# A cross-attention kernel's prologue: queries ahead of keys, x in three pieces, products of the identity, unit 0's maxima drawn together

## The chip, the cores and the metric

The kernel runs on one core of one Trainium2 chip. The metric is the device time of one launch in microseconds (us); of several runs the median is given. A profile is one execution taken by the hardware profiler. TensorE (PE) does matrix products, VectorE (DVE) and ScalarE (ACT) work on vectors, GpSimd (POOL) does elementwise work, SyncE (SP) issues DMAs. PEld is TensorE's weight load.

## The reference, cut to what matters

Two layers of cross attention are applied one after the other to x (32 sequences of 256 rows, 320 channels), each with its own weights. The context has 77 rows of 512 channels per sequence and is the same for both layers. The object, other and image-prompt slices of the reference start past row 77, so they are empty here and add nothing.

```python
q = _split_heads(hidden_states @ Wq.T, H)          # 20 heads of 16
k = _split_heads(text @ Wk.T, H)
v = _split_heads(text @ Wv.T, H)
out = _merge_heads(_attend(q, k, v, 1 / 4))        # softmax over 77 keys
return out @ Wo.T + bo + residual
```

Everything is in float32.

## The kernel before, in words

The work is cut into 32 units: 16 pairs of sequences times two layers, in the order of `units_in_order`. The first four units are layer 0 of pairs 0 to 3. Channels lie on partitions: x of a pair is a tile of 128 x 1280, channels 0 to 127 of both sequences in the first 512 columns, channels 128 to 255 in the next 512, and the last 64 channels of both sequences in the last 256 columns. A unit's 20 heads are handled in five groups (`of_group`).

For each unit the kernel makes:

- `keys` (L215) and `keys_rest` (L236): K transposed, in three banks of PSUM, moved to the tile kT by VectorE (L229) and ScalarE (L253), from which GpSimd makes kM (L256)
- `queries` (L258): the first 256 output channels in four banks. `last_channels` adds the products of the last 64 input channels and `main_channels` those of the first 256; ScalarE copies the banks to q0 (L268). `queries_rest` (L270) does the last 64 output channels and then copies q0 to q1 with a DMA from SP (L277)
- `maxima` (L319), once per group: products of queries and keys into four banks (psm), whose greatest entries VectorE reduces (L334, four reduces) into the tile max
- `turn` (L341): VectorE transposes the maxima (L343), and eight small DMAs (L347) write them into rows of q0 (e = 0, four DMAs) and q1 (e = 1, four DMAs), so that the next products take them off by themselves
- `scores` (L353), once per group: the products that need those rows (pss, L360, first q0, then q1), and the exponential on ScalarE (L366)
- `vals` (L284), `place_vals` (L302): V for a chunk of 128 context rows, and DMAs that put it where a unit needs it
- `values` (L409), `turn_back` (L412), `finish` (L428), `finish_rest` (L436): products with V, division, the output projection, bias and residual

The order of instructions on every engine is the order in which the program issues them. It is written out by hand: the function `at` puts a step in a slot and under a name, and L497 to L501 walk the slots, in each slot in the order load, maxima, turn, scores, values, rest, back, full, last. Unit u's scores start at slot 5u. Before them come its keys (slot s - 8, for unit 0 s - 9), queries (s - 9), keys_rest (s - 7), values (s - 6, s - 5), queries_rest (s - 5), maxima (s - 6 to s - 2) and turn (s - 2), with s = 5u. For units 0 and 1 these slots interleave in the prologue, slots -10 to 0, which is the stretch that the change touches.

Loads: SP's queue takes the context of unit 0, x of pair 0, and later context chunks, x and weights. ACT's queue takes the key, query and value weights of layer 0 (L131). All PSUM tiles come from one pool of eight banks, used in turn: a bank is taken again when the tile eight allocations back has been read. x has seven buffers, so the loads of the first pairs wait for no buffer. DMAs that SP or ACT issues stand in that engine's order of instructions[...].

The identity (L139, L140) is made by GpSimd before anything else is computed; VectorE makes the masks from it (L158 to L166).

Of the kernel before, what the change touches and what calls it, by code (L numbers as in the profile page):

```python
# [53 lines left out]
B, S, C, CA, L = 32, 256, 320, 512, 77  # L54
HEADS, HD = 20, 16
P = 128
NB = 2
NT = NB * S
NX = 2 * NT + S
# [9 lines left out]
PARTS, WIDE = {}, 0  # L69
# [21 lines left out]
def xattn_kernel(ctx: ExitStack, tc: tile.TileContext, xT, cT, cP, weights, outT):  # L91
    nc = tc.nc
# [10 lines left out]
    def bank(name):  # L103
        return psum.tile([P, 512], F32, tag="bank", name=name)
# [2 lines left out]

    def load_x(p):
        x_sb = io.tile([P, NX], F32, tag="x", name=f"x_{p}", bufs=AHEAD + 3)
        nc.sync.dma_start(out=x_sb, in_=xT[p])  # L110
        xs[p] = x_sb

    def load_context(u):
        p = units[u][0]
        c_sb = cs[u] = io.tile([P, NKA, NB * L], F32, tag="c", name=f"c_{u}", bufs=3)
        nc.sync.dma_start(out=c_sb, in_=cP[:, p])
# [10 lines left out]
    def load_weights(layer, first, last, queue):  # L127
        a = PARTS[first][0]
        at, rows, width = PARTS[last]
        b = at + rows * width  # L130
        queue.dma_start(out=w_sb[layer]["all"][:, a:b], in_=weights[layer][:, a:b])  # L131


    load_context(0)
    load_weights(0, "k", "k", nc.scalar)
    load_x(0)
    load_weights(0, "q", "q22", nc.scalar)

    ident = const.tile([P, P], F32, name="ident")  # L139
    make_identity(nc, ident)  # L140
# [23 lines left out]
    for e in range(2):  # L164
        i = HD * (1 - e)
        nc.vector.tensor_scalar_mul(less[:, e : e + 1], r32[:, i : i + 1], -1.0)  # L166

    st = [{} for _ in units]

# [13 lines left out]
    def last_channels(ps, w2, x, **flags):  # L183
        for t in range(2):
            for b in range(NB):
                r = slice(64 * b, 64 * b + 64)
                by_columns(
                    ps[t][b][:, 0:S], w2[r, 0, t * P : (t + 1) * P], x[r, 2 * NT : NX], **flags
                )

    def main_channels(ps, w, x, start, stop):
        for t in range(2):
            for kc in range(2):
                for b in range(NB):
                    i = kc * NT + b * S
                    by_columns(
                        ps[t][b][:, 0:S], w[:, kc, t * P : (t + 1) * P], x[:, i : i + S],
                        start=(start and kc == 0), stop=(stop and kc == 1),
                    )
# [15 lines left out]
    def keys(u):  # L215
        p, layer = units[u]
        w, c_sb = w_sb[layer], cs[u]
        kT = st[u]["k"] = work.tile([P, 2, NG, L], F32, tag="kT", name=f"kT_{u}", bufs=3)
        for t in range(2):
            ps = bank(f"psk_{u}_{t}")  # L220
            for kc in range(NKA):
                by_columns(
                    ps[:, 0 : 2 * L],
                    w["k"][:, kc, t * P : (t + 1) * P],
                    c_sb[:, kc, :],
                    start=(kc == 0),
                    stop=(kc == NKA - 1),
                )
            nc.vector.tensor_tensor(  # L229
                kT[:, :, 2 * t : 2 * t + 2].rearrange("p e g k -> p e (g k)"),  # L230
                ps[:, 0 : 2 * L].unsqueeze(1).broadcast_to([P, 2, 2 * L]),
                masks.unsqueeze(2).broadcast_to([P, 2, 2 * L]),
                ALU.mult,
            )

    def keys_rest(u):  # L236

        p, layer = units[u]
        w, c_sb = w_sb[layer], cs[u]
        kT = st[u]["k"]  # L240
        ps = bank(f"psk_{u}_2")
        for kc in range(NKA):
            for i in range(4):
                b, m = i // 2, i % 2
                nc.tensor.matmul(  # L245
                    ps[32 * i : 32 * i + 32, 0:L],
                    w["k"][:, kc, 2 * P + 32 * m : 2 * P + 32 * m + 32],
                    c_sb[:, kc, b * L : (b + 1) * L],
                    start=(kc == 0),
                    stop=(kc == NKA - 1),  # L250
                )
        for e in range(2):
            nc.scalar.activation(kT[:, e, 4], ps[:, 0:L], AF.Copy, scale=masks[:, e : e + 1])  # L253
        kM = st[u]["km"] = work.tile([P, 2, NG, L], F32, tag="kM", name=f"kM_{u}", bufs=3)
        for e in range(2):
            nc.gpsimd.tensor_scalar_add(kM[:, e], kT[:, e], less[:, e : e + 1])  # L256

    def queries(u):  # L258
        p, layer = units[u]
        w = w_sb[layer]  # L260
        q0, _ = st[u]["q"] = [
            work.tile([P, NX], F32, tag=f"q{e}", name=f"q{e}_{u}", bufs=3) for e in range(2)
        ]
        ps = [[bank(f"psq_{u}_{t}_{b}") for b in range(NB)] for t in range(2)]
        last_channels(ps, w["q2"], xs[p], start=True, stop=False)
        main_channels(ps, w["q"], xs[p], start=False, stop=True)
        for g in range(4):
            nc.scalar.copy(of_group(q0, g), ps[g // 2][g % 2][:, 0:S])  # L268

# [49 lines left out]
    def maxima(u, g):  # L319
        q0, kT, mx = st[u]["q"][0], st[u]["k"], maxes[u % 2]  # L320
        q = of_group(q0, g)
        ps = [bank(f"psm_{u}_{g}_{j}") for j in range(4)]
        for c in range(S // P):
            for j in range(4):
                r = slice(32 * j, 32 * j + 32)
                nc.tensor.matmul(  # L326
                    ps[j][:, c * 2 * L : (c + 1) * 2 * L],
                    q[r, c * P : (c + 1) * P],
                    kT[r, :, g, :],
                    start=True,  # L330
                    stop=True,
                )
        for j in range(4):
            nc.vector.tensor_reduce(  # L334
                mx[:, 2 * g : 2 * g + 2, 2 * j : 2 * j + 2],
                ps[j][:, : 4 * L].rearrange("p (c e k) -> p c e k", e=2, k=L),
                AX.X,
                ALU.max,
            )

    def turn(u):  # L341
        mT = work.tile([P, 2 * NG * 32], F32, tag="mT", name=f"mT_{u}", bufs=2)
        nc.vector.transpose(mT, maxes[u % 2].rearrange("p k i -> p (k i)"))  # L343
        for e in range(2):
            q = st[u]["q"][e].rearrange("(j i) n -> i j n", i=32)[HD * (1 - e)]
            for a in range(P // 32):
                nc.sync.dma_start(  # L347
                    out=q.rearrange("j (k a n) -> a j k n", a=P // 32, n=32)[a],
                    in_=mT[32 * a + e : 32 * a + 8 : 2].rearrange("j (k n) -> j k n", n=32),
                )  # L350
# [98 lines left out]
    def at(slot, where, step):  # L449
        place.setdefault((slot, where), []).append(step)  # L450

    made = [0, 0]
    for u, (p, layer) in enumerate(units):
        s = NG * u
        if layer == 0 and u > 0:
            at(s - 14, "load", lambda p=p: load_x(p))
        if u > 0:
            at(s - 12, "load", lambda u=u: load_context(u))
        at(s - 8 if u else s - 9, "rest", lambda u=u: keys(u))
        at(s - 9, "last", lambda u=u: queries(u))  # L460
        at(s - 7, "rest", lambda u=u: keys_rest(u))
        need = range(p * NB * L // P, ((p + 1) * NB * L - 1) // P + 1)
        when = s - 6
        for i in need:
            if i < made[layer]:
                at(when, "full", lambda u=u, i=i: place_vals(u, i))
                continue
            at(when - 3, "load", lambda layer=layer, i=i: load_chunk(layer, i))
            at(when, "full", lambda layer=layer, i=i: vals(layer, i))
            at(when, "full", lambda u=u, i=i: place_vals(u, i))  # L470
            made[layer] += 1
            when = s - 5
        at(s - 5, "rest", lambda u=u: queries_rest(u))
        for g in range(NG):
            at(s - 6 + g, "maxima", lambda u=u, g=g: maxima(u, g))
            at(s + g, "scores", lambda u=u, g=g: scores(u, g))
            at(s + g + 1, "values", lambda u=u, g=g: values(u, g))
            at(s + g + 1, "back", lambda u=u, g=g: turn_back(u, g))
        at(s - 2, "turn", lambda u=u: turn(u))
        if u < NU - 2:  # L480
            at(s + NG + 1, "full", lambda u=u: finish(u))
            at(s + NG + 3, "rest", lambda u=u: finish_rest(u))
        else:

            slot = NG * NU - (u == NU - 2)
            at(slot, "full", lambda u=u: finish(u))
            at(slot, "last", lambda u=u: finish_rest(u))


    at(-10, "load", lambda: load_weights(0, "v", "v", nc.scalar))  # L490
# [106 lines left out]
```

## Time and profile before

| | |
|---|---|
| median of three runs | 999.02 us (992.94, 999.02, 1000.55) |
| the profiled execution | 995.15 us, its span 993.4 us |
| TensorE busy | 977.5 us of the span, 98% |
| VectorE, ScalarE, GpSimd busy | 590.9, 421.7, 182.7 us |
| first product on TensorE | at 5.65 us |
| first scores of unit 0 | at 37.62 us (first half), 39.89 us (second half) |
| mean granted TensorE clock | 0.995 |
| DMA share, 5 to 10 us and 35 to 40 us | 1.03 and 0.05 |

How to read the lines below. In lists of waits, `A <- B: sum, times, longest` says that instructions A stood still until B had ended. In the chain of work that ended last, each line has a start, a duration and the group of instructions that the chain runs through; "SPq" is the issue of a DMA by SP, "DMA q<-mT" the time until such a transfer had landed, and x64 counts records, of which an fp32 product has two. In tables by window, the stretch is followed by its length, the busy time of the engine asked for, the granted clock, the share of time in which the DMA engines were busy, and the GB/s that they moved. `L173` is the helper that splits a product by columns, so the tile's name (psk, psq, psv, psy) tells keys, queries, values and output apart.

### The profile page before, as it was taken

The page shows a single profiled execution, that of the slowest core. Times are in us where ns is not written, and L with a number is a line of the kernel's source. Part 1 is how long each engine was busy: PE and PEld are TensorE (multiplying, and loading weights), DVE is VectorE, ACT ScalarE, POOL GpSimd, SP SyncE. Part 2 cuts the span into 40 slices and gives each one's busy share as a digit, 9 for nine tenths or more (in the row PEclk, how much of TensorE's full clock was granted, in tenths as well). Part 3 has the DMA queues.
Part 4 walks back from the last instruction along what each step waited for, and adds up shares of the span by engine and source line. Part 5 has one row for each costly group of instructions (what it writes and reads, how often), then busy time and mean ns, then how long its engine had stood idle before and what let it go on. Part 6 is the DMA issues. An engine that isn't in the chain of part 4 may idle for free.

```text
span 993.4 us, 43878 instructions
## 1 busy us (share of the span) xinstructions
PE 977.5 (98%) x19664; PEld 609.0 (61%) x19664; DVE 590.9 (59%) x1380; ACT 421.7 (42%) x905; POOL 182.7 (18%) x236
## 2 busy tenths in 40 slices
PE   7899999999999999999999999999999999999988
PEld 4566665666666666665666666666666666666644
DVE  2466555666655665655666656666556656556654
ACT  1344343454444443444444444444444534444442
POOL 2122201221202222112222112221022221122211
PEclk9999999999999999999999999999999999999989
DMA  6541222221132411223212232311323111231111
GB/s 213 177 160 37 74 79 97 70 77 62 57 122 70 132 47 60 92 80 122 71 44 85 68 123 70 122 34 53 121 80 119 50 62 54 69 107 48 58 47 54
DMA packets 53949, 83.59 MB, mean 84 GB/s; under 512 B 15556, under 2 KB 35652, under 8 KB 53762
## 3 DMA queue, kind: packets, MB, share of 16 engines
q1 hardware_dynamic: 53330, 78.96, 23.9%
q8 instruction: 154, 2.52, 1.0%
q10 hardware_dynamic: 432, 1.84, 0.5%
q14 instruction: 33, 0.27, 0.1%
HBM read 35.39 MB, written 10.49 MB: 46 GB/s over the span
## 4 chain that ended last, share of the span: by engine, by line
PE 97%; DVE 1%; DMA 1%; SPq 1%; issue 0%; POOL 0%; DVEq 0%; POOLq 0%
PE po L380 16%; PE pss L360 15%; PE psy L173 14%; PE psq L173 14%; PE psm L326 12%; PE psv L173 8%; PE psk L173 7%; PE psq L212 4%; PE psy L212 4%; PE psk L245 2%; SPq L347 1%; DVE max L334 1%; DMA w<-in_w_dram 0%; DMA q<-mT 0%; DVE mT L343 0%
## 5 line engine op out<-in xcount | busy, mean ns | idle before, releaser
L366 ACT ACTIVATE pT<-pss 77x512 f32<-77x512 f32 x640 | 326.9, 590 | 242.1 <-PE pss L360 242.1
L334 DVE TENSOR_REDUCE max<-psm 128x4 f32<-128x308 f32 x640 | 259.4, 466 | 172.1 <-PE psm L326 172.1
L401 POOL TENSOR_TENSOR normal<-turned,inv 128x256 f32<-128x256 f32 x160 | 99.3, 621 | 763.9 <-DVE inv L396 763.9
L360 PE MATMUL pss<-q,kM 32*77 32x256 f32 x2560 | 180.6, 380 | 5.8 <-DMA q<-mT 5.8
L380 PE MATMUL po<-pT,v 77*32 77x256 f32 x2560 | 174.0, 389 | 1.0 <-DVE max L334 1.0
L173 PE MATMUL psy<-oT,w 128*32 128x256 f32 (+1 forms) x3072 | 149.4, 380 | 0.0
L173 PE MATMUL psq<-x,w 128*32 128x256 f32 (+1 forms) x3072 | 149.4, 380 | 0.0
L392 DVE STREAM_TRANSPOSE turned<-po 128x512 f32<-128x512 f32 x160 | 113.3, 708 | 46.0 <-PE po L380 42.9
L268 ACT COPY q<-psq 128x256 f32<-128x256 f32 x128 | 47.6, 372 | 213.3 <-PE psq L173 209.5
L326 PE MATMUL psm<-kT,q 32*128 32x154 f32 x2560 | 129.1, 314 | 0.0
L360 PEld LDWEIGHTS pss<-q,kM 32*77 32x77 f32 x2560 | 114.4, 142 | 23.4 <-issue 10.6
L326 PEld LDWEIGHTS psm<-kT,q 32*128 32x128 f32 x2560 | 91.9, 183 | 55.3 <-issue 41.7
L380 PEld LDWEIGHTS po<-pT,v 77*32 77x32 f32 x2560 | 67.5, 110 | 90.3 <-DVE max L334 58.4
L415 DVE STREAM_TRANSPOSE oT<-normal 128x256 f32<-128x256 f32 x160 | 70.9, 443 | 84.5 <-POOL normal L401 81.4
L173 PEld LDWEIGHTS psq<-x,w 128*32 128x32 f32 (+1 forms) x3072 | 85.4, 109 | 57.6 <-issue 14.4
L173 PEld LDWEIGHTS psy<-oT,w 128*32 128x32 f32 (+1 forms) x3072 | 82.2, 108 | 61.2 <-issue 13.2
L422 DVE SCALAR_TENSOR_TENSOR x<-psy,w,x 128x256 f32<-128x256 f32 x160 | 68.6, 479 | 62.8 <-PE psy L173 56.4
L173 PE MATMUL psv<-w,cv 128*32 128x320 f32 x1232 | 93.5, 433 | 0.0
L256 POOL TENSOR_SCALAR kM<-kT,less 128x385 f32<-128x385 f32 x64 | 79.9, 1260 | 38.8 <-ACT kT L253 38.6
L173 PE MATMUL psk<-c,w 128*32 128x154 f32 x2048 | 75.2, 299 | 5.6 <-DMA w<-in_w_dram 5.6
L173 PEld LDWEIGHTS psk<-c,w 128*32 128x32 f32 x2048 | 67.0, 112 | 12.8 <-DMA w<-in_w_dram 5.6
L173 PEld LDWEIGHTS psv<-w,cv 128*32 128x32 f32 x1232 | 41.0, 110 | 40.6 <-issue 1.9
(24 smaller groups left out, 328.3 us busy)
## 6 DMA issues: line engine op xcount, KB each, us to landing
q<-q SPq DMA_DIRECT2D x32, 640.0 KB
x<-in_xT_dram SPq DMA_DIRECT2D x16, 640.0 KB
c<-in_cP_dram SPq DMA_DIRECT2D x32, 308.0 KB
cv<-in_cT_dram SPq DMA_DIRECT2D x38, 256.0 KB
out_dram<-x SPq DMA_DIRECT2D x15, 640.0 KB
v<-stage SPq DMA_DIRECT2D x26, 192.5 KB
q<-mT SPq DMA_DIRECT2D x256, 5.0 KB
w<-in_w_dram ACTq DMA_DIRECT2D x2, 640.0 KB
```

What stands on the lines that cost most here:

```text
L173: nc.tensor.matmul(out[m : m + 32], lhsT[:, m : m + 32], rhs, **flags)
L212: nc.tensor.matmul(ps[r, 0:S], lhsT, rhs, start=(kc == 0), stop=(kc == 2))
L256: nc.gpsimd.tensor_scalar_add(kM[:, e], kT[:, e], less[:, e : e + 1])
L326: nc.tensor.matmul(ps[j][:, c * 2 * L : (c + 1) * 2 * L], q[r, c * P : (c + 1) * P], kT[r, :, g, :], start=True, stop=True,)
L334: nc.vector.tensor_reduce(mx[:, 2 * g : 2 * g + 2, 2 * j : 2 * j + 2], ps[j][:, : 4 * L].rearrange("p (c e k) -> p c e k", e=2, k=L), AX.X ...
L360: nc.tensor.matmul(ps[j][:L, e * S : (e + 1) * S], kM[r, e, g, :], q[r, :], start=True, stop=True,)
L366: nc.scalar.activation(st[u]["p", g][j][:L], ps[j][:L], AF.Exp, scale=SCALE)
L380: nc.tensor.matmul(po[32 * j : 32 * j + 32, e * S : (e + 1) * S], vpad[:L, b, pair, e].rearrange("p a d -> p (a d)"), pT[j][:L, e * S : (e ...
L392: nc.vector.transpose(turned[:, 0 : 2 * S], po)
L401: nc.gpsimd.tensor_tensor(normal.rearrange("p q e d -> p e q d"), outs, inv.unsqueeze(3).broadcast_to([P, 2, S // 32, HD]), ALU.mult,)
L415: nc.vector.transpose(of_group(st[u]["o"], g), normal)
L422: nc.vector.scalar_tensor_tensor(x, ps[:, 0:S], w_sb[layer]["b"][:, 0, t : t + 1], x, ALU.add, ALU.add)
```

## The change

The change is confined to the prologue.

1. x of pair 0 is loaded first, on SP, in three pieces by columns (512, 512, 256), ahead of the context of unit 0. On ACT the query weights come first, in three pieces (two rows of 320 columns, then the rest), and the key weights behind them. x of pair 1 is issued by ACT instead of SP.
2. Four products of the identity with itself go to a bank of their own that nothing reads.
3. Unit 0's queries come before its keys (slot -10, then keys and keys_rest in slot -9), and in them the last channels come after the main ones.
4. Unit 0's maxima of groups 0 to 4 go from slots -6, -5, -4, -3, -2 to -6, -5, -4, -4, -3, and its turn from -2 to -3. Unit 1's keys and keys_rest go from slots -3 and -2 to -4, its queries from -4 to -3, behind the turn.
5. Of unit 0's eight small DMAs in `turn`, the last of each four is issued by ACT.

```diff
+        if p == 0:
+            for a, b in ((0, NT), (NT, 2 * NT), (2 * NT, NX)):
+                nc.sync.dma_start(out=x_sb[:, a:b], in_=xT[p, :, a:b])
+        else:
+            (nc.scalar if p == 1 else nc.sync).dma_start(out=x_sb, in_=xT[p])
...
+    load_x(0)
+    first, _, _ = PARTS["q"]
+    for i in range(2):
+        n = slice(first + i * C, first + (i + 1) * C)
+        nc.scalar.dma_start(out=w_sb[0]["all"][:, n], in_=weights[0][:, n])
+    load_weights(0, "q2", "q22", nc.scalar)
     load_context(0)
     load_weights(0, "k", "k", nc.scalar)
-    load_x(0)
-    load_weights(0, "q", "q22", nc.scalar)
...
+    warm = bank("warm")
+    for _ in range(4):
+        nc.tensor.matmul(warm[:, 0:P], ident, ident, start=True, stop=True)
...
-        last_channels(ps, w["q2"], xs[p], start=True, stop=False)
-        main_channels(ps, w["q"], xs[p], start=False, stop=True)
+        if u == 0:
+
+            main_channels(ps, w["q"], xs[p], start=True, stop=False)
+            last_channels(ps, w["q2"], xs[p], start=False, stop=True)
+        else:
+            last_channels(ps, w["q2"], xs[p], start=True, stop=False)
+            main_channels(ps, w["q"], xs[p], start=False, stop=True)
...
-                nc.sync.dma_start(
+                queue = nc.scalar if u == 0 and a == 3 else nc.sync
+                queue.dma_start(
...
-        at(s - 8 if u else s - 9, "rest", lambda u=u: keys(u))
-        at(s - 9, "last", lambda u=u: queries(u))
-        at(s - 7, "rest", lambda u=u: keys_rest(u))
+        if u > 1:
+            at(s - 8, "rest", lambda u=u: keys(u))
+            at(s - 9, "last", lambda u=u: queries(u))
+            at(s - 7, "rest", lambda u=u: keys_rest(u))
...
+            if u > 0:
+                at(s - 6 + g, "maxima", lambda u=u, g=g: maxima(u, g))
...
+        if u > 0:
+            at(s - 2, "turn", lambda u=u: turn(u))
...
+    at(-10, "last", lambda: queries(0))
+    at(-9, "rest", lambda: keys(0))
+    at(-9, "rest", lambda: keys_rest(0))
+    for slot, g in ((-6, 0), (-5, 1), (-4, 2), (-4, 3), (-3, 4)):
+        at(slot, "maxima", lambda g=g: maxima(0, g))
+    at(-3, "turn", lambda: turn(0))
+    at(-4, "rest", lambda: keys(1))
+    at(-4, "rest", lambda: keys_rest(1))
+    at(-3, "last", lambda: queries(1))
```

More of the change, by code (lines that the diff above doesn't have):

```diff
@@ L109, in load_x @@
         x_sb = io.tile([P, NX], F32, tag="x", name=f"x_{p}", bufs=AHEAD + 3)
-        nc.sync.dma_start(out=x_sb, in_=xT[p])
         xs[p] = x_sb
+        if p == 0:
[3 more added lines that the diff above has]
+            (nc.scalar if p == 1 else nc.sync).dma_start(out=x_sb, in_=xT[p])
     def load_context(u):
@@ L474, in xattn_kernel @@
         for g in range(NG):
-            at(s - 6 + g, "maxima", lambda u=u, g=g: maxima(u, g))
+            if u > 0:
+                at(s - 6 + g, "maxima", lambda u=u, g=g: maxima(u, g))
             at(s + g, "scores", lambda u=u, g=g: scores(u, g))
@@ L478, in xattn_kernel @@
             at(s + g + 1, "back", lambda u=u, g=g: turn_back(u, g))
-        at(s - 2, "turn", lambda u=u: turn(u))
+        if u > 0:
+            at(s - 2, "turn", lambda u=u: turn(u))
         if u < NU - 2:
```

## The prediction, made before the changed kernel was run

> **What bounds the kernel now.** I read the page first, then TensorE's waits over the whole span, then the chain of work that ended last from 0 to 60 us, then windows of 1 and 2 us for the DMA rate and the granted clock. The page's busy times:
>
> ```profile
> PE 977.5 (98%) x19664; PEld 609.0 (61%) x19664; DVE 590.9 (59%) x1380; ACT 421.7 (42%) x905; POOL 182.7 (18%) x236
> ```
>
> TensorE is idle for 993.4 - 977.5 = 15.9 us in all, and the change removes none of its work. Its waits (sum, times, longest):
>
> ```profile
> PE pss L360 <- DMA q<-mT: 5.8, 4, 1.7
> PE psk L173 <- DMA w<-in_w_dram: 5.6, 1, 5.6
> PE po L380 <- DVE max L334: 1.0, 2, 0.8
> ```
>
> So the gain can come from the 5.6 us ahead of the first product and from the first scores' waits for the maxima. Asked for 0 to 45 us alone, the waits give two of those four, 3.1 us, to the prologue; the other two lie in the tail, which is not changed. The chain shows both places (start, us, what):
>
> ```profile
> 5.65 4.34 PE psk L173 x64
> 9.98 4.76 PE psq L173 x96
> ...
> 23.36 4.61 PE psq L173 x96
> ...
> 28.72 2.24 PE psk L173 x64
> 30.96 0.77 PE psm L326 x16
> 31.73 1.63 DVE max L334 x4
> 33.38 0.52 DVE mT L343
> 33.96 0.65 SPq L347
> ...
> 38.15 1.65 DMA q<-mT
> ...
> 39.89 0.67 PE pss L360 x8
> ```
>
> Unit 0's keys take 4.34 us and unit 1's, the same instructions, 2.24; with the queries (4.76 against 4.62) the start pays 2.2 us for a slow array. And from the last maxima (30.96) to the second half of the first scores (39.89) runs a chain: reduce, transpose, eight issues on SP of 0.58 each, a landing. TensorE's work beside it runs out at about 36.1.
>
> The DMA rate at the start (length, weight loads, clock, DMA share, GB/s):
>
> ```profile
> 2.00:3.00 1.00, 0.00 (x0) 1.00 0.81 161
> 3.00:4.00 1.00, 0.00 (x0) 1.00 0.97 387
> ```
>
> And the granted clock in the tail, right after the 2.7 us of waits there (length, PE busy, clock, DMA share, GB/s):
>
> ```profile
> 962.00:964.00 2.00, 1.45 (x12) 0.65 0.80 328
> 964.00:966.00 2.00, 2.00 (x20) 0.50 0.00 0
> ```
>
> [...] the slow products last from 5.65 to about 9.9, 4.25 us, though the clock column reads 1.00 there; in the tail the column itself shows the half clock for some 10 us after two waits. [...] both queues together move 387 to 444 GB/s from 3 to 6 us.
>
> **Part 1, queries first, x in pieces.** Added: two more issues on SP (0.4 each) and two on ACT (0.45), all before 2.5 us, beside the wait for the first bytes. What the first product now needs is 256 KB of x and 160 KB of weights, 426 thousand bytes, instead of the keys' weights (655) served beside the context and x (1,257 moved by 5.60). The windows give 37 + 161 = 198 by 3.0 and 387 per us after: 3.6 us. Landing: between 0 (the two queues share by bytes) and 0.65 us (they share row by row) late, by how well each fits the 5.60 of the keys' weights. I take 4.2[...]. Later pieces: 852 thousand bytes at 4.7 to 5.3, needed after the first quarter of the main products, 2 x 0.86 = 1.7 us at half clock, at 5.9; the last piece (1,180) at 5.4 to 6.1, needed after 8. Keys' weights: 655 and as much from SP's queue on top, 2,490 at 410 GB/s: 8.6 to 9.2; needed after the queries, at 10.2 by the sum below. The queries hide them; without that cover each us late is a us. x_1 moves to ACT behind unit 0's four copies (0.40 each, ending near 11.8), lands by 14 and is needed at 25. Values' weights follow the keys' as before.
>
> **Part 2, products of the identity.** No trace of them. Eight records (an fp32 product has two) of 128 columns over the full width: four column tiles of 256 take 0.216 us at full clock (3.45 us / 64 x 4), so one record takes 0.108, or 0.216 at half: 1.7 us from 1.85, when the identity is made, to 3.6. If no weight load hides (0.183 for 128 columns in psm's row, twice that at half clock): 4.6 us, to 6.5. I take 3.7, ahead of the first x. What they bring is the clock's release: 4.25 us after their start as in this trace, at 6.1; or, if they or the gap to 4.2 count for nothing, 4.2 + 4.25 = 8.45. I take 6.9. Half clock from 4.2 to 6.9 costs 1.35 us (range 1.0 to 2.1) instead of 2.2.
>
> Sum up to the end of unit 0's keys: 4.2 + 4.62 + 2.24 + 0.54 (keys_rest) + 1.35 = 12.95, against 15.28 (14.74 + 0.54): 2.3 us earlier.
>
> **Part 3, maxima close together, turn one slot earlier.** TensorE then has maxima, values, maxima, rest, values (0.74 + 2.29 + 0.74 + 1.43 + 2.15) to 20.3, two maxima to 21.8, unit 1's keys and rest to 24.55, the fifth maxima there. Before, SP's first issue came 3.0 after that start: now 27.55. Bank reuse holds nothing: the closest pair, unit 1's keys on the third maxima's banks, needs reduces that end at 21.5 and 22.0 for starts at 21.8 and 22.9. Behind it stand now unit 1's queries, which moved past it: 0.74 + 4.61 + 0.74 + 2.29 + 0.74 = 9.1 us of work to the scores at 33.65, and 0.43 to their second half. The chain needs 3.0 + issues + 1.65: with all eight on SP 9.3, just hidden; with six, 8.15 (32.7 against 34.1). So 3.09 us of waits go to 0, and the split to ACT (part 4) is worth nothing by itself, up to 1.2 us if the chain runs late. Context c_2 now queues behind the turn on SP (31.1 instead of 26.07); it is needed near 46.8. The loads of slot -4 go out near 21.4; before they took 24.06 to 31.0 with c_2 (1,758 thousand bytes), now 1,443, done near 27, ahead of the turn.
>
> **Part 4, two issues on ACT** wait there for mT until 27.55 and take 1.2. Queued behind them: the copies of unit 1's queries, the first at 28.7 to 29.1; who waits is the maxima at 29.9. 0.8 us of cover, then one for one.
>
> **Total:** 2.3 + 3.1 = 5.4 us. The profiled execution took 995.15 with its span of 993.4: 989.7. The runs shown are 992.94, 999.02 and 1000.55. Their spread looks like clock events: the windows of the tail lose (1 - 0.65) x 2 + 0.5 x 8 + 0.21 x 2 = 5.1 us of clock, so none, one or two such events give about 990, 995 and 1000. The second place with such a gap (0.67 us busy in 3.8) is the first scores' wait, which goes. The median run would then lose 5.4 and one event as well, and come to 988.5; so I keep 989.7.
>
> **Rivals.** (1) *Likeliest, 0.50*: as summed, 989.7, own range 986 to 993. (2) *The spread has another cause, 0.25*: same gains on the median, 999.02 - 5.4 = 993.6. For it: no clock loss is seen after the prologue's gap in this trace. (3) *The tail's event stays away in the median run too, 0.10*: 989.7 - 5.1 = 984.6. Against it: the tail is the same code. (4) *It does only part, 0.13*: the products don't release the clock (8.45, a loss of 0.75), or their loads hold TensorE to 6.5, and the scores wait again: 2.5 us left, 992.7 to 996.5. (5) *Slower than before, 0.02*: the keys' weights, now third in ACT's queue, come so late[...] Against it: everything queued ahead of and beside them is drained by about 10.
>
> **Numbers.** A difference under about 1% can't be told from none here, and 1% below 999.02 is 989.0, inside the likeliest case's own range: 0.4 of its 0.50, all of (3) and a little of the rest give 0.34 for faster; 0.02 for slower; 0.64 between. Range 984.5 to 996.5: from (3) to the upper end of (4).
>
> **What would show it.** First query product near 4.2, with four identity products before it; full-pace products (unit 0's keys near 2.3 us) by 7; end of keys_rest near 13; SP's six issues from 27.5; the scores at 33.6 without a wait; TensorE's idle time near 11.5. Wrong if the first product starts past 5.5, if keys take over 3 us, if a wait for q<-mT is left before 60 us, or if the clock falls to half outside the tail.

## The result and the profile after

The changed kernel takes 991.9 us (median of 20 runs, 987.25 to 994.74); the kernel before takes 995.32 (20 runs, 992.84 to 1000.55). The ratio is 0.9944, 95% interval 0.9928 to 0.9960: some 5.6 us of 1,000 by the ratio, 4.9 by the two means (991.06 and 995.99), 3.4 by the medians. The three differ because the runs of both kernels scatter over 7 us; the experiments below show why. The profiled execution of the changed kernel took 993.09 us, with a span of 991.3.

The page's busy times:

```profile
PE 981.8 (99%) x19672; PEld 611.8 (62%) x19672; DVE 591.1 (60%) x1380; ACT 421.2 (42%) x905; POOL 182.7 (18%) x236
```

TensorE is busier (981.8 us against 977.5) although only eight records were added, two for each identity product: 16 records of scores in the tail take 2.00 us where the clock is at 0.50 and 1.10 where it is at 1.00, and count as busy all the while. Its idle time fell from 15.9 to 9.5 us. Its waits over the span:

```profile
PE pss L379 <- DMA q<-mT: 2.6, 2, 1.5
PE warm L179 <- POOL ident masks.py:199: 1.9, 1, 1.9
PE po L399 <- DVE max L352: 1.0, 2, 0.8
PE psq L186 <- DMA w<-in_w_dram: 0.4, 1, 0.4
PE psm L344 <- ACT q L286: 0.2, 1, 0.2
```

The wait of 5.6 us for the first load is gone (now 1.9, for the identity). Of the four waits for q<-mT the two of the prologue are gone; the 2.6 us left are the tail's. Two small new ones stand below. The chain that ended last, 0 to 45 us (start, us, what):

```profile
4.34 6.56 PE psq L186 x96
10.90 2.24 PE psk L186 x64
13.14 0.54 PE psk L258 x32
13.68 0.74 PE psm L344 x16
14.41 2.78 PE psv L186 x32
...
25.68 0.61 PE psm L344 x13
...
28.77 1.44 ACTq L366
...
31.26 0.81 PE psm L344 x16
32.06 2.29 PE psv L186 x32
34.35 0.74 PE psm L344 x16
35.09 0.89 PE pss L379 x16
```

The first query product comes at 4.34 us, the keys run at full pace (2.24 us, before 4.34), and unit 0's first scores go through in one piece, 35.09 to 35.98. Before, they ended at 40.56: 4.6 us earlier up to there. From there to the end of the last maxima both kernels do the same, and take 912.3 and 912.2 us (all fourteen profiles: 912.2 to 912.7), so what separates the runs lies in the prologue and in the tail. Two things are less than forecast: the first values take 2.78 us instead of 2.29, and the maxima at 31.26 wait for ACT.

Yet the two profiled executions differ by only 995.15 - 993.09 = 2.1 us. The rest was lost at the other end: behind the last maxima the changed kernel took 43.0 us and the kernel before 40.6. The reason is the tail's clock (length, PE busy, clock, DMA share, GB/s):

```profile
956.00:958.00 2.00, 0.48 (x12) 0.78 0.24 85
958.00:960.00 2.00, 2.00 (x20) 0.50 0.62 251
```

It stays at 0.50 up to 974.17, 17.07 us, where the kernel before had it for 10.24.

### The profile page after: what moved, and what is told of

Its sections match the earlier page's. It is cut to its first block, busy times and chain, and to the rows that moved or that the text cites. A ratio compares the mean times of both kernels' runs of the same rounds, so it can differ in the third digit from the quotient of the medians.

```text
span 991.3 us, 43904 instructions
## 1 busy us (share of the span) xinstructions
PE 981.8 (99%) x19672; PEld 611.8 (62%) x19672; DVE 591.1 (60%) x1380; ACT 421.2 (42%) x905; POOL 182.7 (18%) x236
## 4 chain that ended last, share of the span: by engine, by line
PE 97%; DVE 1%; DMA 1%; SPq 0%; issue 0%; ACTq 0%; POOL 0%; ACT 0%; DVEq 0%; POOLq 0%
PE po L399 16%; PE pss L379 15%; PE psy L186 14%; PE psq L186 14%; PE psm L344 12%; PE psv L186 9%; PE psk L186 7%; PE psq L225 4%; PE psy L225 4%; PE psk L258 2%; SPq L366 0%; DMA w<-in_w_dram 0%; DVE max L352 0%; ACTq L366 0%; DMA q<-mT 0%
## 5 line engine op out<-in xcount | busy, mean ns | idle before, releaser
L186 PE MATMUL psk<-c,w 128*32 128x154 f32 x2048 | 73.2, 294 | 0.0
```

What stands on the lines that cost most here:

```text
L186: nc.tensor.matmul(out[m : m + 32], lhsT[:, m : m + 32], rhs, **flags)
```

## The experiments

All times are medians; "before" in a ratio is the kernel before, run on the same chip beside them. e1 to e4 ran on one chip, e5 to e7 on a second, f1 to f4 on a third and f5 on a fourth.

The clock scatters between runs (its mean is 0.990 to 0.998 in the 20 of the changed kernel), so a second measure helps: the span of a run times its mean granted clock, averaged over the runs. It is an estimate of the span at full clock. For the kernel before it gives 987.7 to 987.9 us on each of the four chips, for the changed kernel 983.3, so the change is worth about 4.5 us by this measure. The other numbers "at full clock" below are made in the same way; those of six or seven runs are good to some 0.4 us.

Single profiles scatter too. The start of the kernel before stands in four profiles (before, e3, e7, f1), and its keys_rest ends between 15.13 and 16.07 us. That of the changed kernel stands in six (the changed kernel, e2, e4, e6, f3, f4), with ends between 13.00 and 14.06. A difference of less than a microsecond between two such ends is therefore no finding. The stretches behind keys_rest repeat much better, as experiments 3 and 4 show.

**1. No identity products (e1).**

```diff
-    warm = bank("warm")
-    for _ in range(4):
-        nc.tensor.matmul(warm[:, 0:P], ident, ident, start=True, stop=True)
```

> The changed kernel without its four identity products. Theory (they bring the clock's release forward): the first query product still comes at 4.3 us, [...]the end of unit 0's keys_rest (13.68 with them) comes 0 to 1.5 us later, at 13.7 to 15.2, and the mean time rises by about 0.7 us. Rival (they bring nothing, since they end before the first x and the release comes as late as without them): the end of keys_rest stays within 0.3 us of 13.7.

990.36 us (6 runs), ratio 0.9940 (0.9917 to 0.9964). The pace of the products changed at 9.5 us (at 8.2 with the identity products), and keys_rest ended at 14.32, 0.64 later, inside the theory's range; but the first values ended at 17.34 against 17.19, and the first scores at 36.12 against 35.98. So in this pair the gain was gone 3 us later. One pair does not show that the products brought full pace forward (f2, without them, has keys_rest at 13.85, inside the range of the six profiles). The times don't tell the two apart, and at full clock both are 983.3 us.

**2. The slots of before (e2).**

```diff
-    for slot, g in ((-6, 0), (-5, 1), (-4, 2), (-4, 3), (-3, 4)):
+    for slot, g in ((-6, 0), (-5, 1), (-4, 2), (-3, 3), (-2, 4)):
-    at(-3, "turn", lambda: turn(0))
-    at(-4, "rest", lambda: keys(1))
-    at(-4, "rest", lambda: keys_rest(1))
-    at(-3, "last", lambda: queries(1))
+    at(-2, "turn", lambda: turn(0))
+    at(-4, "last", lambda: queries(1))
+    at(-3, "rest", lambda: keys(1))
+    at(-2, "rest", lambda: keys_rest(1))
```

> The changed kernel with the slots of before for unit 0's maxima and turn and unit 1's keys and queries; loads, identity products, queries first and the two issues on ACT stay. Theory (the new slots are what hides the turn): the waits for q<-mT come back, about 2 us of them in the prologue (3.1 less the two issues' 1.2), and unit 0's first scores end near 38 us instead of 35.98. Rival (the split over two queues alone hides it): under 0.7 us of waits, scores before 36.7.

994.88 us (22 runs), ratio 0.9982 (0.9970 to 0.9994): with the old slots most of the gain is gone by the ratio, and 2.3 of the 4.5 us at full clock (985.6). The first scores ended at 39.00, where some 38 was expected: the halt of experiment 9 took 1.5 us here. The waits of the prologue, which the view puts down to other work:

```profile
PE pss L379 <- DVE max L352: 1.2, 1, 1.2
PE pss L379 <- POOL kM L269: 1.1, 1, 1.1
```

The 2.3 us are the expected size. The names mislead: unit 0's scores don't read the kM that GpSimd had just made for unit 1. SP's last issue for the turn ended at 36.98, and the second half of the scores started at 38.33, 1.35 us behind it (1.20 in the kernel before); kM ended at 38.24, just ahead, and was named as the latest event. That the scores waited for the landing is read from this, not tried.

**3. The slots alone, on the kernel before (e3).** The same lines of the slots as in the change, nothing else of it.

> The kernel before with only the new slots: loads, keys ahead of queries, eight issues on SP and no identity products as before. Theory: the start is that of before (first product 5.65 us, keys_rest ends near 15.3), the waits for q<-mT in the prologue fall from 3.1 us to under 0.5, the first scores end near 37.6 instead of 40.56: 3 us faster than before. Rival (the gain came from the start, and the waits return as something else): under 1.5 us faster.

990.58 us (6 runs), ratio 0.9937 (0.9921 to 0.9953), by the ratio as good as the whole change; at full clock 984.5 us, 1.2 slower than it. First product at 5.83, keys_rest to 15.13, no wait for q<-mT left in the prologue, first scores to 36.70: 3.9 us earlier than before. From the end of keys_rest to the end of the first scores it takes 21.57 us, the kernel before 25.28, and the same two numbers come back in f1 and e7. So the slots are worth 3.7 us there. Of that, 3.1 are the waits; another 0.4 comes from the scores themselves, since two halves of 0.67 us each, apart, take longer than one run of 0.94.

**4. Unit 0's turn whole on SP (e4).**

```diff
-                queue = nc.scalar if u == 0 and a == 3 else nc.sync
+                queue = nc.sync
```

> The changed kernel with all eight issues of unit 0's turn on SP. Theory (the split is worth nothing by itself, since unit 1's queries cover the chain): the last landing moves 1.2 us later and is still within 0.6 us of the scores' start; the 0.2 us wait for the copies behind ACT's issues goes; first scores end between 35.7 and 36.6, time within 0.5 us of the changed kernel's. Rival (the split is needed): the scores wait over 1 us.

991.56 us (7 runs), ratio 0.9947 (0.9928 to 0.9966). First scores to 35.62, no wait for the turn or for the copies. From the end of keys_rest to there it takes 21.56 us; with the split it takes 21.80 where nothing halts (e1, e5, f2). The split is worth nothing and costs 0.24 us, which is too little for the times to show.

**5. x and the query weights whole (e5).**

```diff
-            for a, b in ((0, NT), (NT, 2 * NT), (2 * NT, NX)):
+            for a, b in ((0, NX),):
-    for i in range(2):
-        n = slice(first + i * C, first + (i + 1) * C)
-        nc.scalar.dma_start(out=w_sb[0]["all"][:, n], in_=weights[0][:, n])
-    load_weights(0, "q2", "q22", nc.scalar)
+    load_weights(0, "q", "q22", nc.scalar)
```

> The changed kernel with x of pair 0 in one transfer and the query weights in one. Theory (pieces let the first products start early): the first query product waits for all 1,180 thousand bytes, so it starts at 5.4 to 6.1 us instead of 4.34; at half clock a part of that is made good, since the release comes at the same moment: keys_rest ends 0.6 to 1.5 us later than 13.68. Rival (the keys' weights set that end, or the clock does): keys_rest ends within 0.3 us of 13.7.

995.36 us (22 runs), ratio 0.9976 (0.9965 to 0.9987). The first product started at 6.72, keys_rest ended at 16.55, the first scores at 38.36: 2.4 us later than in the changed kernel. keys_rest came 2.9 us later where 0.6 to 1.5 were expected: the first product was expected at 5.4 to 6.1, and full pace did not come at the same moment but at 11.6 us instead of 8.2. TensorE had been idle from 3.9 to 6.7, and its queries, most of them at half pace, took 7.06 us (unit 1's take 4.61 in the kernel before). Whole loads with queries first start later than the kernel before (5.65), and at full clock (985.2 us) do no better than the slots alone (984.5). What the order of queries and keys brings by itself was not tried.

**6. The tail filled (e6: the changed kernel, e7: the kernel before).** The eight products compute nothing that is read.

```diff
         for e in range(2):
+            if u == NU - 1 and g == 0:
+                fill = bank(f"fill_{e}")
+                for _ in range((3, 5)[e]):
+                    nc.tensor.matmul(fill[:, 0:P], ident, ident, start=True, stop=True)
             q = of_group(st[u]["q"][e], g)
```

> The changed kernel with eight identity products in the tail (three ahead of the first half, five ahead of the second half of unit 31's first scores, where TensorE waits for the last turn). Theory (the spread of the runs is the clock falling to half after those waits): the granted clock stays at 0.998 or above in nearly all runs, the times gather near 987.5 us with a spread under 1.5 us, about 3.5 us under the changed kernel's mean. Rival (the spread has another cause): mean and spread stay (991, 987 to 995).

> The kernel before with the same eight products in its tail. Theory: its times gather near 992.5 us, 5 us above those of the changed kernel with the same filling, which is then the change's worth without the tail's noise (4.6 us by the two profiles up to the first scores, plus what the prologue's waits cost in clock, if anything). Rival: the difference of the two filled kernels is under 3 us, so that part of the 5 us was luck with the clock.

986.25 us (985.71 to 987.42, 5 runs) and 991.38 us (991.27 to 991.67, 6 runs); ratios to the kernel before 0.9895 (0.9876 to 0.9914) and 0.9944 (0.9925 to 0.9962). Both lie 1.1 to 1.3 us below what was expected. Eight products that do no work save 6.2 us in the kernel before (997.60 beside e7) and 5.7 in the changed one (by its 991.9), and the scatter of 7 us is gone. The same stretch of the tail in e6, with the clock full:

```profile
956.00:958.00 2.00, 1.96 (x18) 1.00 0.14 44
```

The two filled kernels are 5.1 us apart: that is the change without the tail's noise. And the kernel e7 still has the prologue's wait, with 0.67 us of work in 2:

```profile
38.00:40.00 2.00, 0.67 (x8) 1.00 0.05 8
```

The clock does not fall there (1.00), and e7's times lie within 0.4 us. So the scatter is the tail's alone.

The traces also show that it comes in steps. In the kernel before the clock changes at 962.61 and 972.85 us, 279 and 282 times 3.413 us behind 10.29, where the products of the start reach full pace; in the changed kernel at 957.10 and 974.17, 278 and 283 times behind 8.20. Below, a piece is such a stretch of 3.41 us, counted from full pace. In the eight profiles whose tail falls, the stretch at 0.50 is two to five pieces long: 6.83 us in e3, e4 and e5 (mean clock 0.997), 10.24 in the kernel before and f4 (0.995), 13.65 in e1 and e2 (0.993), 17.07 in the changed kernel (0.991). By an estimate from this, one piece at half clock costs 1.7 us and 0.0017 of the mean clock, so clocks of 0.998 to 0.988 are one to seven pieces. Here are the two pieces of the prologue's wait in the kernel before, the piece ahead of the fall in its tail, and the fall (length, PE busy, clock, DMA share, GB/s):

```profile
34.19:37.60 3.41, 1.94 (x36) 1.00 0.06 11
37.60:41.02 3.42, 1.80 (x28) 1.00 0.21 55
959.20:962.61 3.41, 0.73 (x12) 1.00 0.19 66
962.61:972.85 10.24, 10.24 (x88) 0.50 0.12 46
```

The prologue's 3.1 us of waits are spread over two pieces and leave each over half busy; the tail's 2.7 us fall into one. The other profiles agree in the main: the pieces ahead of the eight falls are busy for 0.7 to 1.9 us (1.65 in the changed kernel), those of the prologue's waits in e7 and e2 for 1.8 to 2.6. The two ranges overlap a little, so busy time alone does not draw the border, and why the clock stays low for two pieces in one run and five in another is open.

**7. Parts, with the tail filled (f1: e3 filled; f2: e1 filled; f3: below).**

> The kernel before with only the new slots, and the eight products in its tail, so that the tail's clock adds no noise. The two filled kernels measured so far stand at 991.38 us (before) and 986.25 (changed), 5.1 apart. Theory (the slots remove the 3.1 us of waits; loads, order and identity products bring the rest at the start): 988.2 us, 3.1 below the one and 2 above the other. Rival (the slots bring nearly all of it): under 987.

> The changed kernel without its four identity products at the start, with the tail filled. In the profiles so far the values of the first chunk end at 17.1 to 17.5 us whether unit 0's keys_rest ends at 13.0, 13.7 or 14.3. Theory (a halt before the values' fifth record takes back what an earlier release of the clock brings): 986.3 us within 0.4, the same as with them. Rival (the products are worth the 0.7 us by which keys_rest came earlier): 987 or more.

f1 986.91 us (986.57 to 987.70, 5 runs), f2 985.53 (985.25 to 986.24, 4 runs); ratios 0.9884 (0.9863 to 0.9904) and 0.9869 (0.9846 to 0.9892). From f1 to f2, on one chip and with ranges apart, the loads, queries first and the split bring 1.4 us. From e7 (991.38) to f1 the medians give the slots 4.5, but on two chips, and the profiles of the two give 3.6. f1 is its rival's number (under 987), not mine: I had given the slots 3.1. f2 came in below both its numbers: without the identity products nothing is lost. Nor is it shown that they cost something: e6 lies 0.7 above f2, but on another chip and with ranges that overlap, and two of its five runs took 3.0 and 3.5 us outside the span where most take 1.8. By the spans the two medians are 984.1 and 983.75.

f3 has x of pair 1 one slot later on ACT:

```diff
-            at(s - 14, "load", lambda p=p: load_x(p))
+            at(s - 14 + (p == 1), "load", lambda p=p: load_x(p))
```

> The changed kernel, tail filled, with the load of x of pair 1 issued by ACT one slot later, behind unit 0's keys_rest, so that the DMA engines are quiet from about 12.3 us to 14.5. Theory (the halt of TensorE at 14.4 to 15.2, put down to nothing that the profile shows, comes from the loads still running): the halt shrinks below 0.2 us, the values end near 16.3 to 16.8 where keys_rest ends by 13.7, and the time is 0.4 to 0.9 us below 986.25. Rival (the halt has nothing to do with that load): it stays, 986.25 within 0.3.

986.03 us (985.84 to 986.52, 5 runs), ratio 0.9874 (0.9851 to 0.9897). In the three windows of 0.2 us from 12.4 to 13.0 us the DMA engines moved 0 GB/s, and the halt of the weight loads stayed, 0.4 us up to 14.73. By this run the load is not its cause; the rival holds.

**8. Another tail (f4).** Real work in the place of the filling, and ACT issues a part of the last turn:

```diff
-                queue = nc.scalar if u == 0 and a == 3 else nc.sync
+                queue = nc.scalar if u == NU - 1 and a == 3 else nc.sync
-            at(s + g, "scores", lambda u=u, g=g: scores(u, g))
+            late = u == NU - 1 and g == 0
+            at(s + g, "rest" if late else "scores", lambda u=u, g=g: scores(u, g))
+    at(NG * (NU - 1), "turn", lambda: keep_busy(3))
```

> The changed kernel with x of pair 1 later as in f3, unit 0's turn whole on SP, two of the last unit's eight issues on ACT, the last unit's first scores behind the values of the unit before, and three identity products ahead of those. Theory (real work in the place of the filling, and a turn that lands 1.2 us sooner): the clock stays full, about 1.5 to 2 us below f3, near 984.2. Rival (the wait moves behind the exponentials and the clock falls): 986 or more, or a spread over 2 us.

990.54 us (6 runs), ratio 0.9915 (0.9893 to 0.9936): 4.5 us slower than f3. The theory falls and its rival holds. TensorE's new wait:

```profile
PE pss L384 <- ACT pT L390: 1.7, 1, 1.7
```

ACT's two issues stand ahead of exponentials in the program and need the last maxima; the scores wait 1.7 us for an exponential, and from 956.3 to 966.5 us the clock is at 0.50. The clock is most of the loss: five of the six runs have a mean of 0.994 to 0.997, and the sixth, at 1.00, took 987.28, 1.25 above f3.

**9. The halt (f5).** In five profiles (the changed kernel, e2, e6, f3, f4) TensorE or its weight loads halted behind the fourth record of the first values.

```diff
+    for _ in range(4):
+        nc.tensor.matmul(warm[0:32, 0:32], ident[:, 0:32], ident[:, 0:32], start=True, stop=True)
```

> The changed kernel, tail filled, with four more identity products of 32 columns behind the four at the start: eight more product records and eight more weight loads on TensorE ahead of all that follows, at a cost well under 1 us before the first x is there. In five profiles TensorE halted behind the fourth record of the first chunk's values, up to 14.7 to 15.2 us, for no reason that the profile shows. Theory (the instructions behind that place in TensorE's program arrive late): the halt moves with the count, eight records earlier, to behind the twelfth record of unit 0's first maxima, and ends in the same stretch, 14.7 to 15.2 us. Rival (the data of that product arrives late): it stays behind the fourth record of the values, or at their first. Time 986.1 us within 0.6 either way.

987.18 us (986.63 to 988.38, 6 runs), ratio 0.9913 (0.9893 to 0.9933), 0.5 us over the upper end of what was expected. TensorE's timeline in e6 (start, us, engine, line, operation, tiles):

```profile
13.77 0.73 PE L186 MATMUL psv<-w,cv 128*32 128x320 f32 x4
14.92 0.74 PE L186 MATMUL psv<-w,cv 128*32 128x320 f32 x8 [0.42 <-issue]
```

and in f5:

```profile
13.26 0.79 PE L346 MATMUL psm<-kT,q 32*128 32x154 f32 x13
14.55 0.53 PE L346 MATMUL psm<-kT,q 32*128 32x154 f32 x3 [0.50 <-issue]
```

With eight more records ahead of it, the halt comes eight records earlier (counted by weight loads: behind the fifth of the values, now behind the thirteenth of the maxima). So, by this one profile, it belongs to a place in TensorE's program, not to a load. "issue" means that the view shows nothing waited for. The list of DMA queues does show, ahead of it, a transfer of a kind that it calls "instruction"; in the changed kernel, from 12.2 to 12.4 us:

```profile
q8 instruction: 1, 0.02, 35.0%
```

It begins between 12.2 and 12.4 there, 12.6 and 12.8 in e2, 12.0 and 12.2 in f5, and TensorE goes on at 14.85, 15.21 and 14.55: about 2.5 us later each time (2.4 to 2.6 in all six profiles with the halt). Where TensorE reaches the place later than that, it runs through: in the kernel before the transfer begins between 13.4 and 13.6, and the values start at 16.02 and take 2.29 us. That this transfer is what TensorE waits for fits these times, but is not shown. Why the transfer starts when it does was not tried.

## Why the prediction was right, and where its steps were off

The sum was 5.4 us; the filled kernels give 5.1 and the spans at full clock about 4.5. Direction and size held, the terms less so. That the sum came out so near is in part luck: the slots brought more than their term, and a halt that no term had took back a part of the start. Nor says it much that 991.9 lies between 984.5 and 996.5, for that range holds the kernel before's own median, 995.32, too.

- *Start (forecast 2.3 us).* The first product was right (4.34 for 4.2). The moment of full pace was not: the products' pace changes at 8.19 us, where I took 6.9, so half clock cost 1.9 us instead of 1.35 (inside the range given, 1.0 to 2.1). keys_rest ended at 13.68 instead of 12.95. The "4.25 us" behind that term was misread and is no constant: in the kernel before the pace changes at 10.3 us, 4.6 behind the first product, and the six profiles that start with no identity products have 3.4 to 5.6. Averaged over profiles, keys_rest ends at 15.60 with the start of before and at 13.47 with that of the change, 2.1 earlier, so the forecast of 2.3 nearly held there. Then the halt, which no step had, cost 0.5: the first values ended at 17.19, against 18.30 before. So 1.1 us of the 2.3 arrived in this profile. (From the end of keys_rest to there it takes 3.0 us where nothing halts and 3.5 to 4.6 where something does.)
- *Identity products.* "What they bring is the clock's release": that was my estimate, which no trace had shown; by these profiles they can, but not always. With them ahead of the queries the pace changes at 6.75 to 8.65 us in seven profiles, without them at 9.5 (e1) and 8.15 (f2). Cut into the pieces of 3.41 us, all fourteen profiles say the same: full pace came behind the first piece in which TensorE was busy for a large share (0.81 in f4, 0.86 in e2, up to 1.00), and a piece with 0.78 (e4) or less brought none. In the changed kernel the piece with most of the identity products, 1.37 to 4.78 us, had 0.74, and full pace came one piece later, when the queries alone had filled it; in e2 the piece from 3.34 to 6.75 had 0.86, of which the queries, from 4.42 on, were 0.68. Where the pieces fall differs from run to run, and with it what the products bring; f2 shows that the kernel is no slower without them. Bringing keys_rest forward ran into the halt: 13.10 in e6, 13.68 in the changed kernel and 13.00 in e2 all gave first values that ended at 17.2 to 17.6.
- *Waits at the scores (forecast 3.1).* The step "maxima close together, turn one slot earlier" was right in mechanism and too small: 3.7 us from keys_rest on, of which 0.4 because the scores no longer run in two halves. The medians of e7 and f1 are 4.5 apart, but their profiled executions 3.6 (991.34 and 987.70), like their first scores; the rest of the 4.5 is not explained. The sum of the chain counts one issue twice, since the landing's 1.65 us run from the start of the last issue: before, the chain took 8.93 us (30.96 to 39.89), not 9.3, so it was hidden with more room than forecast.
- *The issues on ACT.* "0.8 us of cover": the first of them took 1.44 us instead of 0.58 and mT came at 28.7 instead of 27.55, so the copies were 0.2 us late and the maxima waited. e4 shows that the split wasn't needed, as forecast.
- *The spread.* Clock events in the tail were right: e6 and e7 show it. A second place in the prologue was wrong: e7 keeps that wait and has no scatter. So the change could not save an event, and rival 2, in which the spread had another cause altogether, was wrong too. Nor were the events of one size: they cost 3.4 to 8.5 us in the profiles, not 5.1. And the waits of the tail left no piece empty: TensorE was busy for 0.7 to 1.9 us of the 3.41 before each fall.
- *The median.* 991.9 lies 2.2 above the 989.7 because the summed execution had a mean clock of 0.995 and the changed kernel's runs at the median have 0.993, one piece of 3.41 us at half clock more. Its 20 spans times their mean clock are 983.3 us within 0.6 (one standard deviation), while the clocks run from 0.990 to 0.998. That the execution summed, 995.15, lay at the later median of 20 and not at the 999.02 of the first three was luck.

The lowest median is that of f2 (new slots, queries first in pieces, no identity products at the start, tail filled): 985.53 us, ratio 0.9869 (0.9846 to 0.9892); the ranges of f3 and e6 overlap with its own. The same with unit 0's turn whole on SP was not run.

## What to carry to other kernels

Look for the waits that come last in a stage and put independent work there: drawing the maxima together, so that the turn could go ahead of other work, brought most of the gain, and the earlier loads and queries 1.2 to 1.4 us more. When runs scatter more than the effect, find the place that scatters (the clock column by windows) and quiet it before comparing. And don't share a queue's issues with an engine whose next work somebody waits for: the maxima waited 0.2 us for it in the changed kernel, the scores 1.7 us in f4.

## What was not expected of the hardware

- Waits of some 2.6 us in the tail cost 3.4 to 8.5 us more through the clock, for 6.8 to 17 us at 0.50 with TensorE busy nearly throughout, in two to five pieces of 3.41 us. With eight products of 128 x 128 in the waits, the profiled executions of e6, e7, f1 to f3 and f5 have a mean clock of 0.999 or 1.000.
- Full pace came 3.4 to 5.6 us behind the first product in the six profiles that have no identity products ahead of it; e3 and f1, which start with the same instructions, have 3.8 and 5.6.
- Two DMA issues on ACT took 1.44 and 0.55 us while SP issued too; on SP alone, in the kernel before, one takes 0.54 to 0.65.
- TensorE halted by up to 0.8 us (its weight loads by 1.4) at what looks like a fixed place of its program, some 2.5 us behind the start of a transfer that the list of queues calls "instruction", with no wait shown.
